# A transformer block on one core: where the projection's products are summed, where the next columns stand, and what a unit's attention waits for

## The chip, the core and the metric

The kernel runs on one core of a Trainium2 chip. The metric is the device time of one execution in microseconds; three runs of the kernel before gave 2201.77 us as the median (2200.89 to 2212.07). All data are 32-bit floats. A product of TensorE (PE in the profile) appears there as two passes, each with its own weight load, so five contraction chunks are "x10".

## The reference

The input `x` is 8 sequences of 512 tokens with 576 features; `cond` is one row of 576 features for each sequence. First the tokens are rotated inside a 64-dimensional subspace: `U` from a QR decomposition of `P`, `R` as the matrix exponential of a skew matrix made from `cond`. Then follows one transformer block whose shifts, scales and gates come from `cond`:

```
x = x + ((x U) R - x U) U^T
ada = silu(c) @ ada_w + ada_b        # six rows of 576: shift, scale, gate, twice
x = x + gate_msa * (attention(modulate(layernorm(x))) @ proj_w + proj_b)
x = x + gate_mlp * mlp(modulate(layernorm(x)))       # 576 -> 2304, gelu, -> 576
```

The attention is unusual: for every token, the 16 heads of that token attend to each other (`einsum('nthd,ntkd->nthk')`), so the scores are 16 x 16 for each token, and no token looks at another. Its result is transposed to heads first and reshaped to rows of 576 before the projection, so a row that is projected mixes 16 tokens of one head.

## The kernel before

**Stages.** A first stage of some 230 us makes the QR decomposition, the exponentials and the modulation. The rest works in 16 **units**, two for each sequence, each of 256 tokens (two tiles of 128). For a unit k the program traces, in this order:

1. `Projection.__init__`: the loads of the projection's weights (L902, L903), of the gathered attention rows `at` (L906) and of the residual rows `x1` (L908), all on SyncE's queue (SP).
2. The **columns** of a later tile: `qkv` gives six pieces for a tile, each a product of 128 tokens with 288 columns over five chunks (L800), copied out of the bank by ScalarE (ACT, L811) and stored to memory (L812). Units 1 to 10 carry the columns of two tiles (12 pieces), units 11 to 14 those of one (6 pieces), unit 15 none; unit 0 carries four pieces. A piece takes its bank from the pool `ps_mm`, which has two.
3. `turn(t)`: five transposes of `at` into banks of `ps_f1`, and two ACT copies to `aT` (L918).
4. `product(t, n)`: four in all, each of five chunks (L928). Before the change their banks also come from `ps_mm`. VectorE (DVE) takes each out with the gate (L930, tile `pt`) and adds it to `x1` (L931).
5. `norm(t)`: statistics on DVE (L137 to L139), a power on GpSimd (POOL, L140), the normalised rows `xn`/`xm` on DVE (L141).
6. `turn_normed`: ten transposes (L946) and five ACT operations that give `h2T` (L949), the input of the MLP.
7. `mlp`: nine steps of fc1 (L973), Gelu on ACT (L981), four sums on POOL (L1029 to L1032; the last is `s3s[g]`), and fc2 (L1044, L1046, L1049) into four banks of `ps_acc`; then nine products into a bank of `ps_f1` (L1059, `p7`); then the **tail**: an ACT copy (L1074), a chain of DVE operations that empties the banks (L1075 to L1087), POOL's additions into `x1` (L989) and the stores `out<-x` (L992). Inside the MLP, `aside` computes the rotation and the transposed input of the sequence two ahead.
8. `ops(40, att)`: all the operations of the attention of unit k+1. Each is a DVE operation on 128 x 2304 elements: eight pairs of product and sum for the scores of both tiles (L838, L845), eight for the values (L866, L873), with a small softmax between.

**What sets the order.** Up to the end of unit 0's projection the orders of PE, DVE and POOL are as the program is written. After that the framework's scheduler makes the order of each engine when the program is built: in its own simulation it gives an engine the earliest traced of the instructions that are ready, and the engines and the SP queue then run these orders strictly. An operation traced late, as the attention's are, so fills any gap that the simulation sees.

**What holds the attention back.** `attention` is a generator. With `after` it first copies one column of some tile into its score tile (L831), so that no sum of scores (L845) can come before that tile exists. Line 1212 gives it `pr.aT[0]`. The lambda is read when the generator starts, which is an iteration later: the attention of unit k+2 waits for `aT[0]` of unit k+1.

```
        if k + 2 < N:
            att = attention(*units[k + 2], after=lambda: pr.aT[0][:, 0, 0:1])
```

**Where the columns stand.** The list of pieces is filled up with `None` in front to twelve entries (L1180). Five stand ahead of `turn(0)`, one between it and `product(0, 0)`, one ahead of each of the other three products, two ahead of the first `turn_normed`, one behind it. A unit with six pieces so has none ahead of `turn(0)` or of `product(0, 0)`.

Of the kernel before, what the change touches and what calls it, by code (L numbers as in the profile page):

```python
# [9 lines left out]
F32 = mybir.dt.float32  # L10
# [14 lines left out]
HALF = D // 2  # L25
# [23 lines left out]
def rotate_then_dit_block(  # L49
# [53 lines left out]
    def srows(c):  # L103
        return 65 if c == 4 else 128
# [47 lines left out]
    with tc.manual_schedule(engines=engines), tc.tile_pool(name="prep", bufs=1) as prep, tc.tile_pool(name="qrs", bufs=2) as qrs, tc.tile_pool(  # L152
        name="ada", bufs=4
    ) as adap, tc.tile_pool(name="exs", bufs=1) as exs, tc.tile_pool(
        name="ps_qr", bufs=1, space=PSUM
    ) as ps_qr, tc.tile_pool(
        name="ps_ex", bufs=2, space=PSUM
    ) as ps_ex, tc.tile_pool(name="ps_m", bufs=2, space=PSUM) as ps_m, tc.tile_pool(
        name="ps_x", bufs=1, space=PSUM
# [374 lines left out]
        t, done = column_products(0), None  # L534
        for j in range(R):
            t, done = qr_step(j, t, done)
# [13 lines left out]
        if True:  # L550
# [43 lines left out]
            for c, rows in enumerate(KROWS):  # L594
                ps = ps_ex.tile([R, 128], F32, tag="ex", name=f"vt_{c}")
# [25 lines left out]
            ps = ps_m.tile([R, R], F32, tag="m", name="s_ps")  # L621
# [38 lines left out]
            for n in range(2):  # L660
                cols = slice(n * HALF, (n + 1) * HALF)
                ps = ps_qr.tile([128, HALF], F32, tag="rp", name=f"first_rot_{n}")
# [9 lines left out]
            for n in range(2):  # L672
                ps = ps_ex.tile([128, HALF], F32, tag="ex", name=f"ut_{n}")
# [15 lines left out]
    ps_mm = ctx.enter_context(tc.tile_pool(name="ps_mm", bufs=2, space=PSUM))  # L689
    ps_f1 = ctx.enter_context(tc.tile_pool(name="ps_f1", bufs=2, space=PSUM))  # L690
    ps_acc = ctx.enter_context(tc.tile_pool(name="ps_acc", bufs=4, space=PSUM))
# [199 lines left out]
    class Projection:  # L891
# [29 lines left out]
        def product(self, t, n):  # L921
            aT, x1 = self.aT[t], x1s[self.hb][t]
            cols = slice(n * HALF, (n + 1) * HALF)
            ps = ps_mm.tile([128, HALF], F32, tag="mm", name=f"pj_{self.hb}_{t}_{n}")
            for c in range(NK):
                k = srows(c)
                w = self.w[n][c // 3][0:k, c % 3]
                nc.tensor.matmul(ps, lhsT=aT[0:k, c, :], rhs=w, start=c == 0, stop=c == NK - 1)  # L928
            tmp = tiles.tile([128, HALF], F32, tag="tmp", name=f"pt_{self.hb}_{t}_{n}", bufs=3)
            nc.vector.tensor_tensor(tmp, ps, self.gate[:, cols], ALU.mult)  # L930
            nc.vector.tensor_tensor(x1[:, cols], x1[:, cols], tmp, ALU.add)  # L931
# [59 lines left out]
    def store(pr, t):  # L991
        nc.sync.dma_start(out=tile_rows(out[pr.b], pr.ts[t]), in_=x1s[pr.hb][t])  # L992
# [20 lines left out]
    def mlp(pr, gate, aside):  # L1013

        hb = pr.hb
        QUARTER = HALF // 2
        gts, sums, s3s = {}, {}, {}
        banks = [ps_acc.tile([128, 512], F32, tag="acc", name=f"fc2_{hb}_{k}") for k in range(4)]
        p = [bank[:, 0:HALF] for bank in banks]
        halves_of = {5: (banks[0], banks[1]), 6: (banks[2], banks[3])}  # L1020
        side = slice(HALF, HALF + QUARTER)
        for g in range(NP + 1):
            if g in aside:
                aside[g]()
            if g < NP:
                gt = gts[g] = fc1(pr, g)
                ss = sums[g] = tiles.tile([128, 3, 128], F32, tag="ss", name=f"ss_{hb}_{g}")
                s3s[g] = tiles.tile([128, 128], F32, tag="s3", name=f"s3_{hb}_{g}", bufs=NP)
                nc.gpsimd.tensor_tensor(ss[:, 0], gt[:, 0, 1], gt[:, 1, 1], ALU.add)  # L1029
                nc.gpsimd.tensor_tensor(ss[:, 1], ss[:, 0], gt[:, 0, 0], ALU.subtract)  # L1030
                nc.gpsimd.tensor_tensor(ss[:, 2], gt[:, 1, 0], ss[:, 1], ALU.subtract)  # L1031
                nc.gpsimd.tensor_tensor(s3s[g], gt[:, 0, 0], gt[:, 0, 1], ALU.subtract)  # L1032
            g -= 1
            if g < 0:
                continue
            wq = wst.tile([128, 3, HALF], F32, tag="w2q", name=f"wq_{hb}_{g}", bufs=3)
            nc.sync.dma_start(out=wq, in_=fc2_q[g])
            wt = wst.tile([128, 3, HALF], F32, tag="w2t", name=f"wt_{hb}_{g}", bufs=3)
            nc.sync.dma_start(out=wt, in_=comb_d[g])
            gt, ss = gts.pop(g), sums.pop(g)  # L1040
            stop = g == NP - 1
            whole = [(gt[:, 0, 0], wq[:, 0]), (gt[:, 1, 0], wq[:, 1]), (ss[:, 2], wq[:, 2]), (gt[:, 1, 1], wt[:, 1])]
            for k in (0, 1, 3):
                nc.tensor.matmul(p[k], lhsT=whole[k][0], rhs=whole[k][1], start=g == 0, stop=stop)  # L1044

            nc.tensor.matmul(p[2], lhsT=whole[2][0], rhs=whole[2][1], start=g == 0, stop=stop)  # L1046
            for i, (lhs, rhs) in ((5, (ss[:, 0], wt[:, 0])), (6, (ss[:, 1], wt[:, 2]))):
                for n, bank in enumerate(halves_of[i]):
                    nc.tensor.matmul(  # L1049
                        bank[:, side],  # L1050
                        lhsT=lhs,
                        rhs=rhs[:, n * QUARTER : (n + 1) * QUARTER],
                        start=False,
                        stop=stop,
                        skip_group_check=True,
                    )
        p7 = ps_f1.tile([128, 512], F32, tag="f1", name=f"p7_{hb}")
        for g in range(NP):
            nc.tensor.matmul(p7[:, 0:HALF], lhsT=s3s[g], rhs=t3[:, g], start=g == 0, stop=g == NP - 1)  # L1059

        def made(tag):
            return tiles.tile([128, HALF], F32, tag=tag, name=f"{tag}_{hb}", bufs=1)

        def add(out_, a, b_, op=ALU.add):

            if isinstance(b_, tuple):
                for n, bank in enumerate(b_):
                    q = slice(n * QUARTER, (n + 1) * QUARTER)
                    nc.vector.tensor_tensor(out_[:, q], a[:, q], bank[:, side], op)
            else:  # L1070
                nc.vector.tensor_tensor(out_, a, b_, op)

        u1, u2, u4 = made("u1"), made("u2"), made("u4")
        nc.scalar.copy(u2, p[0])  # L1074
        nc.vector.tensor_tensor(u1, u2, p[1], ALU.add)  # L1075
        finish(hb, 0, 0, u1, gate)
        add(u2, u2, halves_of[6])
        add(u4, u2, halves_of[5])
        nc.vector.tensor_tensor(u4, u4, p[2], ALU.add)
        finish(hb, 0, 1, u4, gate)  # L1080
        store(pr, 0)
        nc.vector.tensor_tensor(u2, u2, p7[:, 0:HALF], ALU.add)
        c21 = made("u1")
        nc.vector.tensor_tensor(c21, u2, p[3], ALU.subtract)
        finish(hb, 1, 0, c21, gate)
        add(u2, u2, halves_of[5])
        finish(hb, 1, 1, u2, gate)  # L1087
        store(pr, 1)

# [2 lines left out]
    units = [(b, (i, i + 1)) for b in range(B) for i in (0, 2)]  # L1094
    N = len(units)

    def now(pieces):
        for piece in pieces:
            if piece:
                piece()  # L1100

    def ops(n, of):
        for _ in range(n):
# [7 lines left out]
    q = qkv(0, 0)  # L1111
# [6 lines left out]
    q = qkv(0, 1)  # L1118
    att = attention(*units[0])
# [33 lines left out]
    q = qkv(1, 3)  # L1153
# [5 lines left out]
    att = attention(*units[1])  # L1159
    ops(6, att)  # L1160

    ahead = {0: [None] * 5 + q[2:3] + [None] * 3 + q[3:]}
    tiles_of = [(unit[0], i) for unit in units[4:] for i in unit[1]]
    for k in range(1, N - 1):
        for tile_ in [tiles_of.pop(0) for _ in range(2 if k < 11 else 1)]:
# [3 lines left out]
    for k, (b, ts) in enumerate(units):  # L1169
        if ts[0] == 0:  # L1170
            gate_a, gate_m = gate_rows(0, b), gate_rows(1, b)
            gb2 = big.tile([128, D], F32, tag="gb2", name=f"gb2_{b}")
            nc.sync.dma_start(out=gb2, in_=fc2_b.to_broadcast([128, D]))
            nc.gpsimd.tensor_tensor(gb2, gb2, gate_m, ALU.mult)
        pr = Projection(b, ts, gate_a)
        q = ahead.get(k, [])
        if k:
            q = [piece for tile_ in q for piece in qkv(*tile_)]

        q = [None] * (12 - len(q)) + q  # L1180
        now(q[:5])
        pr.turn(0)
        now(q[5:6])
        pr.product(0, 0)
        pr.turn(1)
        now(q[6:7])
        pr.product(0, 1)
        pr.norm(0, gb2)
        now(q[7:8])
        pr.product(1, 0)  # L1190
        now(q[8:9])
        pr.product(1, 1)
        pr.norm(1, gb2)
        if k == 0:
            ops(1, att)
        now(q[9:11])
        pr.turn_normed((0, 1))
        now(q[11:])
        pr.turn_normed((2, 3))
        pr.turn_normed((4,))  # L1200
        if k == 0:
            held.close()
        aside = {}
        if b + 2 < B:
            if ts[0] == 0:
                coming = rotation(b + 2)
            p = coming[:3] if ts[0] == 0 else coming[3:]
            aside = {1: p[0], 3: p[1], 5: p[2], 8: lambda: feature_major(b + 2, ts[0] // 2)}
        mlp(pr, gate_m, aside)
        ops(40, att)  # L1210
        if k + 2 < N:
            att = attention(*units[k + 2], after=lambda: pr.aT[0][:, 0, 0:1])


# [49 lines left out]
```

## Time and profile before

| | us |
|---|---|
| median of three runs | 2201.77 |
| the profiled execution, its own time | 2205.87 |
| its span, first to last instruction | 2204.2 |
| from unit 0's projection on (365 to 2204) | 1839, of which PE is busy 1788.3 |
| period of two units with 12 pieces (L1059 at 960.41, at 1199.29 two units later) | 238.9 |
| period of two units with 6 pieces (L1059 at 1676.76, at 1889.22) | 212.5 |
| one product or one piece (x10, L928 or L800) | about 2.43 |
| one attention operation on DVE (L838, L845, L866, L873) | 2.54 to 2.61 |
| DVE busy in the MLP and projection of one unit (965 to 1083) | 99.2 of 118 |

Shares of busy time: PE 95%, DVE 82%, POOL 32%, ACT 20%. TensorE's granted clock is full from 382 us on, but for seven stretches of 3.4 us at half of full speed in units 12 to 15.

How to read it: in a chain or a timeline, a bracket behind a group gives the idle time ahead of it and what ended that. The number behind a wait is its sum in us, how often it occurred, and the longest.

### The profile page before, as it was taken

How to read it: one execution, taken by the hardware profiler on the slowest of the kernel's cores; microseconds unless marked ns; L12 is line 12 of the kernel's file. 1: busy time of each engine (PE TensorE's matmuls, PEld its weight loads, DVE VectorE, ACT ScalarE, POOL GpSimd, SP SyncE). 2: the span in 40 equal slices, each digit the busy share in tenths (PEclk: the TensorE clock that was granted, in tenths of full speed). 3: DMA queues.
4: the chain of work that ended last, by engine and by line, in shares of the span. 5: the costliest groups of instructions: out<-in, count | busy, mean ns of one | idle time of the engine just before them, and what ended most of it. 6: DMA issues, size and time to landing. Idle time of an engine off the chain costs nothing.

```text
span 2204.2 us, 27929 instructions
## 1 busy us (share of the span) xinstructions
PE 2090.5 (95%) x10087; PEld 1679.3 (76%) x10087; DVE 1801.2 (82%) x2544; ACT 434.9 (20%) x922; POOL 714.1 (32%) x918
## 2 busy tenths in 40 slices
PE   6996998999999999999999999999999999999988
PEld 3475666887878787888878787878787878787867
DVE  8997599788879696969697887969698989896930
ACT  2232221212121111212121212111121212111110
POOL 2341243242424151424333242415142323232422
PEclk9855799999999999999999999999999999999999
DMA  8202265485848576666848484857667676675754
GB/s 272 86 2 73 90 207 158 147 244 160 250 136 244 154 233 191 190 192 199 233 146 252 151 254 132 243 156 230 193 188 221 198 197 184 183 220 166 201 175 124
DMA packets 239789, 400.79 MB, mean 182 GB/s; under 512 B 85502, under 2 KB 127435, under 8 KB 239652
## 3 DMA queue, kind: packets, MB, share of 16 engines
q1 hardware_dynamic: 213732, 372.46, 57.5%
q10 hardware_dynamic: 25920, 26.55, 3.6%
q8 instruction: 80, 1.31, 0.3%
q14 instruction: 57, 0.47, 0.1%
HBM read 340.01 MB, written 58.94 MB: 181 GB/s over the span
## 4 chain that ended last, share of the span: by engine, by line
PE 66%; issue 13%; DVE 9%; POOL 4%; DMA 4%; ACT 3%; SPq 0%; ACTq 0%; POOLq 0%; DVEq 0%
PE fc L973 28%; PE fc L1044 9%; PE qkvp L800 8%; PE fc L1049 6%; PE fc L1046 3%; PE p L1059 2%; PE pj L928 1%; ACT h2T L949 1%; DMA out<-x 1%; DVE sc L845 1%; PE zps L730 1%; PE dp L270 1%; DMA gate<-gates_d 1%; PE ada L352 1%; PE htr L773 1%
## 5 line engine op out<-in xcount | busy, mean ns | idle before, releaser
L973 PE MATMUL fc<-h2T,w 128*128 128x256 f32 (+1 forms) x2880 | 656.5, 382 | 7.3 <-ACT h2T L949 7.2
L973 PEld LDWEIGHTS fc<-h2T,w 128*128 128x128 f32 (+1 forms) x2880 | 542.1, 192 | 83.6 <-ACT h2T L949 11.6
L800 PE MATMUL qkvp<-wqkv,hT 128*128 128x288 f32 (+1 forms) x1920 | 494.1, 412 | 23.6 <-DVE pt L930 15.0
L800 PEld LDWEIGHTS qkvp<-wqkv,hT 128*128 128x128 f32 (+1 forms) x1920 | 365.7, 192 | 130.0 <-DVE pt L930 18.3
L838 DVE TENSOR_TENSOR qk<-qkv 128x2304 f32<-128x2304 f32 x128 | 334.6, 2614 | 12.1 <-DMA qkv<-tok 8.6
L1029 POOL TENSOR_TENSOR ss<-gt 128x128 f32<-128x128 f32 x144 | 155.0, 1076 | 548.3 <-ACT gt L981 548.3
L866 DVE TENSOR_TENSOR pv<-sc,qkv 128x2304 f32<-128x2304 f32 x128 | 330.4, 2581 | 1.8
L873 DVE TENSOR_REDUCE att<-pv 128x144 f32<-128x2304 f32 x128 | 325.8, 2545 | 2.4
L845 DVE TENSOR_REDUCE sc<-qk 128x64 f32<-128x2304 f32 x128 | 325.4, 2543 | 1.7
L981 ACT ACTIVATE gt<-fc 128x512 f32<-128x512 f32 x144 | 86.0, 597 | 649.1 <-PE fc L973 636.5
L811 ACT COPY qs<-qkvp 128x288 f32<-128x288 f32 x180 | 71.9, 399 | 516.7 <-PE qkvp L800 471.1
L1049 PEld LDWEIGHTS fc<-wt,ss 128*128 128x128 f32 x1152 | 160.6, 190 | 15.1
L1049 PE MATMUL fc<-wt,ss 128*128 128x144 f32 x1152 | 164.7, 286 | 0.0
L1044 PE MATMUL fc<-wq,gt 128*128 128x288 f32 x576 | 163.2, 405 | 0.0
L140 POOL TENSOR_TENSOR rstd_m<-rstd_m,mhalf 128x1 f32<-128x1 f32 x32 | 19.6, 613 | 439.4 <-DVE rstd_m L139 369.8
L1044 PEld LDWEIGHTS fc<-wq,gt 128*128 128x128 f32 x576 | 107.5, 189 | 22.7
L1075 DVE TENSOR_TENSOR u<-u,fc 128x288 f32<-128x288 f32 x16 | 7.3, 454 | 136.5 <-ACT u L1074 136.5
L928 PE MATMUL pj<-w2q_p,aT 128*128 128x288 f32 x384 | 104.2, 406 | 0.9 <-ACT aT L918 0.9
L1046 PE MATMUL fc<-wq,ss 128*128 128x288 f32 x288 | 94.1, 408 | 3.2 <-POOL ss L1031 3.2
L1030 POOL TENSOR_TENSOR ss<-ss,gt 128x128 f32<-128x128 f32 x144 | 95.9, 666 | 0.0
L1044 PE MATMUL fc<-wt,gt 128*128 128x288 f32 x288 | 93.4, 406 | 0.0
L831 DVE COPY sc<-aT 128x1 f32<-128x1 f32 x14 | 2.1, 152 | 109.4 <-ACT aT L918 109.4
(254 smaller groups left out, 2393.9 us busy)
## 6 DMA issues: line engine op xcount, KB each, us to landing
w<-in_fc_w SPq DMA_DIRECT2D x288, 320.0 KB
wq<-in_fc_q SPq DMA_DIRECT2D x144, 432.0 KB
wt<-comb_d SPq DMA_DIRECT2D x144, 432.0 KB
tok<-qs ACTq DMA_DIRECT2D x180, 144.0 KB
qkv<-tok SPq DMA_DIRECT2D x30, 864.0 KB
w2q_p<-in_proj_w SPq DMA_DIRECT2D x32, 432.0 KB
xT<-in_x_t SPq DMA_DIRECT2D x16, 640.0 KB
xt<-in_x SPq DMA_DIRECT2D x32, 288.0 KB
```

Source lines behind the costliest of these rows:

```text
L800: nc.tensor.matmul(ps, lhsT=hT[0:k, c, i * 128 : (i + 1) * 128], rhs=wqkv[0:k, c, cols], start=c == 0, stop=c == NK - 1,)
L838: nc.vector.tensor_tensor(pr, q[:, c * HC : (c + 1) * HC].unsqueeze(2).to_broadcast([128, HC, H, DH]), k.unsqueeze(1).to_broadcast([128, H ...
L845: nc.vector.tensor_reduce(sc[t][:, c * HC : (c + 1) * HC, :], pr, AX.X, ALU.add)
L866: nc.vector.tensor_tensor(pr, sc[t][:, c * HC : (c + 1) * HC, :].unsqueeze(2).to_broadcast([128, HC, DH, H]), v.unsqueeze(1).to_broadcast( ...
L873: nc.vector.tensor_reduce(att[:, c * HC : (c + 1) * HC, :], pr, AX.X, ALU.add)
L928: nc.tensor.matmul(ps, lhsT=aT[0:k, c, :], rhs=w, start=c == 0, stop=c == NK - 1)
L973: nc.tensor.matmul(ps[:, k], lhsT=w1[0:n, c, :], rhs=h2T[0:n, c, 0 : NU * 128], start=c == 0, stop=c == NK - 1,)
L1029: nc.gpsimd.tensor_tensor(ss[:, 0], gt[:, 0, 1], gt[:, 1, 1], ALU.add)
L1030: nc.gpsimd.tensor_tensor(ss[:, 1], ss[:, 0], gt[:, 0, 0], ALU.subtract)
L1044: nc.tensor.matmul(p[k], lhsT=whole[k][0], rhs=whole[k][1], start=g == 0, stop=stop)
L1046: nc.tensor.matmul(p[2], lhsT=whole[2][0], rhs=whole[2][1], start=g == 0, stop=stop)
L1049: nc.tensor.matmul(bank[:, side], lhsT=lhs, rhs=rhs[:, n * QUARTER : (n + 1) * QUARTER], start=False, stop=stop, skip_group_check=True,)
```

## The change

Three things change.

- The four products of a projection take their banks from `ps_acc`, the pool of four banks that fc2 accumulates in, not from `ps_mm`.
- The pieces of columns are placed by count: all but the last eight ahead of `turn(0)` (four of 12, none of 6), one ahead of `product(0, 0)`, none between the four products, all but one of the rest ahead of the first `turn_normed` (six of 12, four of 6), the last behind it. Unit 0 keeps the order it had.
- `mlp` returns its list `s3s`, and the attention of unit k+2 waits for `s3s[6]` of unit k's MLP: the fourth POOL sum of the seventh of its nine steps.

```
-            ps = ps_mm.tile([128, HALF], F32, tag="mm", name=f"pj_{self.hb}_{t}_{n}")
+            ps = ps_acc.tile([128, 512], F32, tag="acc", name=f"pj_{self.hb}_{t}_{n}")[:, 0:HALF]
...
-    ahead = {0: [None] * 5 + q[2:3] + [None] * 3 + q[3:]}
+    ahead = {0: q[2:]}
...
-        q = [None] * (12 - len(q)) + q
-        now(q[:5])
+        front = max(0, len(q) - 8)
+        now(q[:front])
         pr.turn(0)
-        now(q[5:6])
+        now(q[front : front + 1])
         pr.product(0, 0)
         pr.turn(1)
-        now(q[6:7])
         pr.product(0, 1)
         pr.norm(0, gb2)
-        now(q[7:8])
         pr.product(1, 0)
-        now(q[8:9])
         pr.product(1, 1)
         pr.norm(1, gb2)
         if k == 0:
             ops(1, att)
-        now(q[9:11])
+        now(q[front + 1 : -1])
         pr.turn_normed((0, 1))
-        now(q[11:])
+        now(q[-1:])
         pr.turn_normed((2, 3))
         pr.turn_normed((4,))
...
-        mlp(pr, gate_m, aside)
+        s3s = mlp(pr, gate_m, aside)
         ops(40, att)
         if k + 2 < N:
-            att = attention(*units[k + 2], after=lambda: pr.aT[0][:, 0, 0:1])
+            att = attention(*units[k + 2], after=lambda s=s3s[6]: s[:, 0:1])
```

`mlp` ends with `return s3s`, and `now` no longer skips empty entries.

More of the change, by code (lines that the diff above doesn't have):

```diff
@@ L1088, in mlp @@
         store(pr, 1)
+        return s3s
     units = [(b, (i, i + 1)) for b in range(B) for i in (0, 2)]
@@ L1098, in now @@
         for piece in pieces:
-            if piece:
-                piece()
+            piece()
     def ops(n, of):
```

## The prediction

> **What bounds the kernel now.** I read the busy shares first, then who waited for whom on PE, then the half-clock stretches, then the timeline of one projection.
>
> ```profile
> PE 2090.5 (95%) x10087; PEld 1679.3 (76%) x10087; DVE 1801.2 (82%) x2544; ACT 434.9 (20%) x922; POOL 714.1 (32%) x918
> ```
>
> PE is the bound: from unit 0's projection on it is busy 1788 of 1839 us. The change removes no product, so only PE's idle time and its slow clock can be won or lost. The waits on PE over the whole span:
>
> ```profile
> engine line waited for: us in total, times, longest us
> ...
> PE qkvp L800 <- DVE pt L930: 15.0, 14, 1.8
> ...
> PE fc L973 <- ACT h2T L949: 7.2, 15, 0.8
> PE h2tr L946 <- DVE xm L141: 6.4, 5, 3.5
> ...
> PE fc L1046 <- POOL ss L1031: 3.2, 6, 0.9
> ...
> PE atr L917 <- DMA at<-att: 2.8, 1, 2.8
> ...
> PE atr L917 <- DVE u L1082: 1.9, 1, 1.9
> ```
>
> The first is the one the change aims at: a piece of columns waits until DVE has taken a product out of one of the two `ps_mm` banks, once in each unit 1 to 14. By stretches, units 1 to 10 wait 0.79 us each and units 11 to 14 1.79 us each (7.9 + 7.2 = 15.1). Units 11 to 14 add waits for `xm` (0.4, 1.1, 1.1, 0.3), and lose clock too; the third number from the end of a windows line is the granted clock (0.92 and 0.84 in unit 13's projection):
>
> ```profile
> 1905.00:1920.00 15.00, 13.21 (x51) 9.93 (x51) 14.55 (x17) 1.20 (x3) 2.10 (x2) 0.92 0.54 168
> 1920.00:1930.00 10.00, 7.64 (x28) 5.46 (x28) 9.45 (x12) 4.80 (x9) 1.96 (x2) 0.84 0.29 87
> ```
>
> Why a bank is taken out late is seen on DVE:
>
> ```profile
> 978.53 0.15 DVE L831 COPY sc<-aT 128x1 f32<-128x1 f32 x1 [10.94 <-ACT aT L918]
> 978.72 2.55 DVE L845 TENSOR_REDUCE sc<-qk 128x64 f32<-128x2304 f32 x1
> 981.31 2.56 DVE L838 TENSOR_TENSOR qk<-qkv 128x2304 f32<-128x2304 f32 x1
> 983.78 0.45 DVE L930 TENSOR_TENSOR pt<-pj,gate 128x288 f32<-128x288 f32 x1
> 984.15 2.54 DVE L845 TENSOR_REDUCE sc<-qk 128x64 f32<-128x2304 f32 x1
> 986.61 0.45 DVE L931 TENSOR_TENSOR x<-x,pt 128x288 f32<-128x288 f32 x1
> 986.97 2.55 DVE L838 TENSOR_TENSOR qk<-qkv 128x2304 f32<-128x2304 f32 x1
> ```
>
> Two things: the copy of L831 holds DVE idle for 10.9 us after the MLP's tail; and once the attention runs, an operation of 2.55 us slips in between two that depend on each other (`pt`, then `x1`).
>
> **The change part by part.** E is the end of the `p7` products.
>
> 1. *Products in `ps_acc`.* They no longer share banks with the pieces, which ACT alone then empties; the five pieces at 964.77 run in 12.31 us with no wait. Units 1 to 10: 10 x 0.79 = **-7.9**. Cost if the cover goes: the four banks must have been emptied by the tail (last read at 967, E + 2; the first product there is at 979.9) and emptied again before fc2, which starts some 9 us behind `h2T`, itself behind the last `pt`. So nothing here.
>
> 2. *Products back to back.* The chain from the last product to its normalised row took 10.6 us in a 12-piece unit (997.6 to 1008.2) and 12.3 in unit 13 (1912.5 to 1924.8). Now more of PE's work stands behind the last product: seven pieces of 2.43 us = 17 us with 12 pieces, which covers the chain; five pieces = 12.2 us with six, which just covers it (unit 11 has 3.5 us of rotation as well). Unit 13 before: E = 1893.4, fc1 starts at 1927.4, E + 34.0. After: 26.5 us of PE work (ten of 2.43 us, two turns of 0.55, ten transposes 1.1) if nothing waits; by the chain: a piece and four products with turns end at E + 14 to 15, + 12.3, + 2.6 from `xm` to fc1 as now = E + 29.5. Gain 4.5, of which 1.8 is the wait for the bank and most of the rest is that the clock stays up.
>    What is there to win in units 11 to 14: bank waits 7.2, `xm` 2.9, `aT` 4 x 0.24 = 0.9, and the half clock: 20 passes of pieces in 6.81 instead of 5.12 us and 40 of fc1 in 10.60 instead of 8.91 (unit 12), about the same in unit 13, 10.44 instead of 8.91 in unit 14: 8.3. Together **19.3**. I take half, **-9.6**, because of part 3.
>
> 3. *Attention from `s3s[6]`.* That sum ends at 1059 where E is 1083: the attention starts some 37 us earlier than now, if the one before has ended. It has: DVE is busy 99 of 118 us a unit, so the hold sets the start and the idle time moves to mid-MLP. The heavy operations now run in the tail: L1075 to L1087 (5.3 us of work on DVE in a dozen operations) get some of them between. Queued behind are POOL's L989, then `out<-x`, and behind that on SP the reload of `x1` (L908 waits for `out<-x` 28 times, 127.6 us). Bounds: no operation more to seven of 2.55 us, 0 to 17.9 us. I take two to three (5 to 7.5 us): several steps are in pairs that need nothing of each other, the `p7` step fills a gap, and the softmax's own small steps fill others. With 12 pieces it is hidden: 9.7 us of pieces and a turn stand ahead of the first product, and `xm` has 3 to 8 us to spare. With six the reload of the second `x1`, issued at 1901.3 (E + 7.9) in unit 13, has 7.4 us until its use at 1911.2 (with 2.5 us for its landing, an estimate between nothing and the 4.6 us that a load three times as large took, 2033.4 to 2038.0), and the turn's fifth transpose waits for L1082 to free `p7` (0.35 us now, up to 2.5 then). This eats the half.
>
> 4. *The last units.* Attention 15 ends at 2101.2, while the tail's ACT copy was done at 2097.3: L1075 is 3.8 us late, PE waits 1.9 us for L1082 and 2.8 us for `at<-att` (2111). It now starts in unit 13's MLP; only its second tile waits, as now, for unit 14's columns (loaded 2033 to 2038). Sixteen operations or 42 us later, 2080, it is done, well ahead. **-4.7**. Between nothing (if both tiles' values also come after the load: 24 operations, 2100) and that.
>
> Added and removed instructions: none on PE or ACT; L831 reads another tile at the same 0.15 us.
>
> Sum: -7.9 - 9.6 - 4.7 = -22.2 on the profiled execution's 2205.9, that is 2183.7; the shown median is 4.1 lower, so the forecast is **2180**.
>
> *A rule against the change.* POOL's sum L1032 takes 448 ns at best, 456 in the median and 2817 at most, the long ones while DVE multiplies; in the last third DVE will multiply. The Trainium skill, "SBUF — State Buffer", section "Who interferes with whom", says that a DVE instruction with two SBUF inputs contends with a GpSimd one that reads SBUF and that a DVE reduction never does; the trace agrees (L1029 takes 2.38 us at 1050.5 under `pv`). It makes the second rival below, whose numbers come from these rows.
>
> **Rivals.**
>
> *Everything is won.* The tail stays short: 15.1 + 2.9 + 0.9 + 8.3 + 4.7 = 31.9, **2170**. For: the sums above. Against: the tail has no cover in six-piece units.
>
> *POOL's sums become the wait.* At the last fc2 step `ss` is needed 4.1 us after Gelu's start (1073.1 to 1077.2) and takes 0.6 + 1.9 us; one multiplication in its way adds up to 2.4, so 0.9 us in each of 15 units: 13. With -7.9 - 4.7 and nothing in six-piece units: about **2202**. For: the six waits of up to 0.9 us on L1031 now. Against: by the order of operations from 1059 on, a multiplication ends near 1074, half a microsecond into the sums, as it does today (0.94 us at 1073.8).
>
> *The attention hardly starts earlier* (loads of its rows, or the order chosen, hold it): parts 1 and a little of 2, **2193**.
>
> *Slower: the tail becomes the path.* Between every two dependent steps of the tail one heavy operation slips in, as in the lines at 983.8. At seven, 17.9 us: the second reload is issued at E + 25.8, `x1` is added at E + 28 instead of E + 17.8, and the 16.3 us from there to fc1 (1911.2 to 1927.4) give E + 44: 10 us more in each of four units, 40 - 7.9 - 4.7 = +27, **2229**. It decides from four to five inserted operations on (4 x (stretch - 7.4) above 12.6, a stretch of 10.5 us). For: that pattern is in every projection. Against: it needs every gap to be filled.
>
> **How the numbers follow.** Forecast 0.45, everything won 0.13, POOL 0.14, no earlier start 0.10, slower 0.18. Half a per cent (11 us) is about what can be told from no change: faster is below 2190.8, slower above 2212.8. Faster: 0.45 + 0.13 = 0.58, the 2193 case on its border; same 0.24; slower 0.18. The forecast's own range is 2168 to 2192 (all or nothing of part 2's half). The range that leaves out 2 in 10 runs from 2165 to 2216: it holds the middle cases and a tail stretched by five operations, not by seven.
>
> **What would show it.** Right: no wait of L800 for `pt`; L831 waits for POOL and not for `aT`, ahead of E by 20 us or more; fc1 of unit 13 starts by E + 30; one half-clock stretch at most in units 12 to 14; no wait for `at<-att` in unit 15. Wrong: more than four heavy operations between L1075 and the last L988 of a tail; the reload of `x1` later than E + 15; a new wait of `h2tr` for `xm` in six-piece units above 4 us; waits of L1046 for `ss` in every unit.

## The result and the profile after

The changed kernel took 2173.2 us in the median of four runs (2170.2 to 2176.1); the kernel before, beside it, 2205.8 us (2200.9 to 2212.1). The ratio is 0.985, with a 95% interval of 0.982 to 0.988: some 33 us faster, where 22 had been forecast. The profiled execution took 2173.5 us with a span of 2171.8, against 2205.9 and 2204.2.

The busy shares of the changed kernel:

```profile
PE 2074.7 (96%) x10087; PEld 1676.4 (77%) x10087; DVE 1825.2 (84%) x2544; ACT 401.4 (18%) x896; POOL 658.7 (30%) x918
```

PE is 16 us less busy with the same 10087 products, part of it by less time at half clock. ACT has 26 instructions less (922 before): all are table loads, 1283 ns each, of which 34 stand beside the softmax (L852) and Gelu (L981) where there were 60. So the prediction's "none on PE or ACT" was wrong for ACT. Every kernel below with the new hold in all units has these 34, and every other has 60; ACT, busy 18% of the span, is not the bound. The waits on PE over the span (us in total, times, longest):

```profile
PE h2tr L946 <- DVE xm L141: 13.1, 12, 3.5
...
PE fc L1046 <- POOL ss L1031: 2.6, 4, 1.6
PE atr L917 <- DMA at<-att: 2.5, 1, 2.5
...
PE fc L973 <- ACT h2T L949: 1.5, 2, 1.3
...
PE atr L917 <- DVE u L1082: 1.2, 1, 1.2
...
PE pj L928 <- DVE u L1079: 0.5, 1, 0.5
```

The first line of before, `qkvp` for `pt`, 15.0 us, is gone altogether. `fc` for `h2T` fell from 7.2 to 1.5. One wait has grown, `h2tr` for `xm`, from 6.4 to 13.1, and it now comes in twelve places instead of five. `at<-att` is still there.

The waits on VectorE show where its idle time went:

```profile
DVE sc L831 <- POOL s L1032: 104.0, 13, 10.4
...
DVE qk L838 <- DMA qkv<-tok: 15.0, 1, 15.0
```

Before, L831 waited 109.4 us in all for `aT`, in ten units just ahead of a projection's products. Now it waits about as long for the POOL sum, in mid-MLP. So most of this idle time is still there, but at another place. The second line has grown: 15 us for one load in unit 14 (8.6 before).

From the start of L1059 in each unit one reads a period for every unit. Summed, in us:

| | before | after | difference |
|---|---|---|---|
| units 1 to 10 (L1059 at 482.93 to 1676.59; after, 481.14 to 1661.86) | 1193.7 | 1180.7 | -12.9 |
| units 11 to 14 (to 2097.47; after, to 2064.12) | 420.9 | 402.3 | -18.6 |
| unit 15 (to 2191.99; after, to 2159.64) | 94.5 | 95.5 | +1.0 |

The 1.8 us that are left lie ahead of unit 0's L1059. That stretch differs by more between executions of one and the same kernel (481.14 here, 485.51 in the repeat below), so nothing is read from it.

The tail in unit 13, where only one piece is traced ahead of the products (start, us, engine, line, operation):

```profile
1870.89 0.45 DVE L1075 TENSOR_TENSOR u<-u,fc 128x288 f32<-128x288 f32 x1
...
1872.81 2.55 DVE L845 TENSOR_REDUCE sc<-qk 128x64 f32<-128x2304 f32 x1
1875.27 0.45 DVE L1079 TENSOR_TENSOR u<-u,fc 128x288 f32<-128x288 f32 x1
...
1876.73 3.02 DVE L838 TENSOR_TENSOR qk<-qkv 128x2304 f32<-128x2304 f32 x1
1879.67 0.45 DVE L988 TENSOR_TENSOR mt<-u,gate 128x288 f32<-128x288 f32 x1
...
1880.46 2.54 DVE L845 TENSOR_REDUCE sc<-qk 128x64 f32<-128x2304 f32 x1
1882.92 0.44 DVE L988 TENSOR_TENSOR mt<-u,gate 128x288 f32<-128x288 f32 x1
```

Three heavy operations have slipped into the tail, the top of the two to three forecast. E is 1873.3; the products run without pieces between them, their last ends near 1886, and fc1 starts at 1903.12, that is E + 29.8 (E + 34.0 before).

### The profile page after: what moved, and what is told of

Same layout as the page of the kernel before. It is cut to its first block, busy times and chain, and to the rows that moved or that the text cites. A ratio compares the mean times of both kernels' runs of the same rounds, so it can differ in the third digit from the quotient of the medians.

```text
span 2171.8 us, 27934 instructions
## 1 busy us (share of the span) xinstructions
PE 2074.7 (96%) x10087; PEld 1676.4 (77%) x10087; DVE 1825.2 (84%) x2544; ACT 401.4 (18%) x896; POOL 658.7 (30%) x918
## 4 chain that ended last, share of the span: by engine, by line
PE 58%; DVE 24%; issue 10%; POOL 4%; DMA 2%; ACT 1%; ACTq 0%; SPq 0%; POOLq 0%; DVEq 0%
PE fc L973 24%; PE fc L1044 8%; PE fc L1049 5%; PE qkvp L800 5%; DVE sc L845 4%; DVE att L873 4%; DVE qk L838 3%; PE fc L1046 3%; DVE pv L866 3%; PE pj L928 2%; PE p L1059 2%; PE zps L730 1%; PE rot L741 1%; PE dp L270 1%; DVE m L325 1%
## 5 line engine op out<-in xcount | busy, mean ns | idle before, releaser
L800 PE MATMUL qkvp<-wqkv,hT 128*128 128x288 f32 (+1 forms) x1920 | 485.0, 410 | 8.0 <-ACT qs L811 5.8
L800 PEld LDWEIGHTS qkvp<-wqkv,hT 128*128 128x128 f32 (+1 forms) x1920 | 364.2, 192 | 110.3 <-ACT qs L811 7.6
L838 DVE TENSOR_TENSOR qk<-qkv 128x2304 f32<-128x2304 f32 x128 | 336.7, 2630 | 18.8 <-DMA qkv<-tok 15.0
L866 DVE TENSOR_TENSOR pv<-sc,qkv 128x2304 f32<-128x2304 f32 x128 | 333.1, 2602 | 2.8
L873 DVE TENSOR_REDUCE att<-pv 128x144 f32<-128x2304 f32 x128 | 326.1, 2548 | 2.6
L1029 POOL TENSOR_TENSOR ss<-gt 128x128 f32<-128x128 f32 x144 | 109.9, 763 | 643.9 <-ACT gt L981 643.9
L981 ACT ACTIVATE gt<-fc 128x512 f32<-128x512 f32 x144 | 86.0, 597 | 769.2 <-PE fc L973 739.9
L989 POOL TENSOR_TENSOR x<-x,mt 128x288 f32<-128x288 f32 x64 | 71.1, 1111 | 211.5 <-DVE mt L988 211.5
L1032 POOL TENSOR_TENSOR s<-gt 128x128 f32<-128x128 f32 x144 | 108.3, 752 | 0.0
L928 PE MATMUL pj<-w2q_p,aT 128*128 128x288 f32 x384 | 104.8, 408 | 0.5 <-DVE u L1079 0.5
L1046 PE MATMUL fc<-wq,ss 128*128 128x288 f32 x288 | 93.9, 408 | 2.8 <-POOL ss L1031 2.6
L831 DVE COPY sc<-s 128x1 f32<-128x1 f32 x14 | 2.1, 153 | 104.0 <-POOL s L1032 104.0
```

What stands on the lines that cost most here:

```text
L800: nc.tensor.matmul(ps, lhsT=hT[0:k, c, i * 128 : (i + 1) * 128], rhs=wqkv[0:k, c, cols], start=c == 0, stop=c == NK - 1,)
L838: nc.vector.tensor_tensor(pr, q[:, c * HC : (c + 1) * HC].unsqueeze(2).to_broadcast([128, HC, H, DH]), k.unsqueeze(1).to_broadcast([128, H ...
L866: nc.vector.tensor_tensor(pr, sc[t][:, c * HC : (c + 1) * HC, :].unsqueeze(2).to_broadcast([128, HC, DH, H]), v.unsqueeze(1).to_broadcast( ...
L873: nc.vector.tensor_reduce(att[:, c * HC : (c + 1) * HC, :], pr, AX.X, ALU.add)
```

## The experiments

The change has three parts: the **banks**, the **columns** and the **hold** (what the attention waits for). All eight combinations of them were run, two kernels that take the columns apart, and three that alter the last unit. A median is compared with that of before in the same group of runs (2207.7, 2205.6 and 2205.7 us). The periods are read as above, each from one profiled execution; a line number behind a tile is that of the kernel shown, and in the kernels with another last order the lines behind the attention stand six further down (L952 is L946).

| kernel | median | ratio to before, 95% interval | units 1-10 | units 11-13 | units 14-15 |
|---|---|---|---|---|---|
| before | 2205.8 | | 1193.7 | 317.8 | 197.6 |
| banks | 2192.8 | 0.994 (0.992 to 0.995) | 1191.0 | 318.3 | 189.5 |
| columns | 2163.6 | 0.981 (0.979 to 0.984) | 1172.3 | 302.0 | 192.7 |
| hold | 2229.7 | 1.011 (1.009 to 1.012) | 1232.3 | 310.7 | 193.0 |
| banks, columns | 2168.3 | 0.983 (0.981 to 0.984) | 1172.3 | 304.2 | 194.0 |
| banks, hold | 2234.5 | 1.013 (1.010 to 1.015) | 1239.7 | 313.6 | 189.9 |
| columns, hold | 2187.9 | 0.991 (0.989 to 0.994) | 1190.5 | 313.1 | 190.5 |
| all three, again | 2173.7 | 0.985 (0.982 to 0.987) | 1180.7 | 307.2 | 190.9 |
| pieces behind only | 2176.0 | 0.987 (0.985 to 0.989) | 1179.6 | 306.7 | 194.6 |
| products together only | 2193.8 | 0.994 (0.993 to 0.996) | 1200.2 | 306.6 | 190.5 |
| all three, last order | 2171.6 | 0.984 (0.982 to 0.987) | 1180.9 | 304.8 | 189.6 |
| banks, columns, hold and order in the last unit only | 2168.0 | 0.982 (0.980 to 0.985) | 1172.3 | 305.7 | 196.9 |
| columns, last order | 2164.0 | 0.982 (0.980 to 0.984) | 1172.2 | 303.9 | 195.6 |

**The banks alone.**

```
-            ps = ps_mm.tile([128, HALF], F32, tag="mm", name=f"pj_{self.hb}_{t}_{n}")
+            ps = ps_acc.tile([128, 512], F32, tag="acc", name=f"pj_{self.hb}_{t}_{n}")[:, 0:HALF]
```

> Only the banks of the four products change (ps_acc in place of ps_mm); the columns stay between the products and the attention waits for aT as before. Theory (cover): the wait of a column for the product's bank (15.1 us in all) goes, but the products and their normalisation chain keep their place, so PE arrives at the transposes of the normalised rows that much earlier and waits there: the h2tr wait for xm grows from 6.4 to some 15 to 20 us, and the time falls by 0 to 5 us only. Rival (banks): the shared banks were the whole cause, the 15 us are won and the time falls by 13 to 17 us.

15.0 us faster, so the total is the rival's. But where it comes from is not what the rival said. In units 1 to 10, where it had 7.9 us to win, the kernel wins 2.7; most of the rest is in the last two units. The waits on PE of this kernel:

```profile
PE h2tr L946 <- DVE xm L141: 24.1, 13, 7.3
...
PE fc L973 <- ACT h2T L949: 5.4, 13, 0.5
...
PE fc L1046 <- POOL ss L1031: 3.0, 7, 0.6
```

The wait for `pt` is gone, and the wait for `xm` went from 6.4 to 24.1 us: PE arrives at `h2tr` earlier and waits there, 0.5 to 1.0 us in each of units 1 to 10 and 18.2 us in units 11 to 15. The theory of cover is right about the mechanism.

**The hold alone**, its line in the diff and `mlp`'s return.

> Only the hold changes: the attention waits for s3s[6], products in ps_mm with columns between them as before. Theory (cover): DVE loses its idle 10.9 us ahead of the projection, but PE's waits for the product's bank stay at 0.8 to 1.8 us a unit; the tail is longer by two to three attention operations; the time lies within 8 us of before. Rival (attention): 15 us or more faster, since DVE's idle time was what the change took away.

22 us slower, which neither theory had. The waits on PE of the hold alone; then from its timeline the products' place on PE, and DVE at the same time:

```profile
PE pj L928 <- DVE pt L930: 21.5, 12, 3.7
...
PE fc L973 <- ACT h2T L949: 7.9, 13, 1.3
PE qkvp L800 <- DVE pt L930: 7.1, 12, 1.4
```

```profile
1246.48 2.59 PE L800 MATMUL qkvp<-wqkv,hT 128*128 128x288 f32 x10
1250.88 1.72 PE L928 MATMUL pj<-w2q_p,aT 128*128 128x288 f32 x6 [1.81 <-DVE pt L930]
```

```profile
1245.13 2.54 DVE L866 TENSOR_TENSOR pv<-sc,qkv 128x2304 f32<-128x2304 f32 x1
1247.59 0.41 DVE L856 TENSOR_REDUCE sm<-sc 128x16 f32<-128x256 f32 x1
1247.91 2.54 DVE L873 TENSOR_REDUCE att<-pv 128x144 f32<-128x2304 f32 x1
1250.37 0.45 DVE L930 TENSOR_TENSOR pt<-pj,gate 128x288 f32<-128x288 f32 x1
```

The product ended at 1246.6 and is taken out at 1250.37, behind two attention operations of 2.54 us each (L866, L873). In the kernel before, VectorE idled 10.94 us for L831 just ahead of the products and took up the attention only 1.4 us before the first of them (978.53 and 979.89). With the hold it works without a gap from mid-MLP through the tail into the products. The spare time is much the same; its place is worse. In units 1 to 10 PE is idle 24.7 us longer than before (40.1 against 15.4) and counts 14.0 us more as busy. Some of the latter is slow clock: this trace has 17.1 us at half clock in these units, where before has none.

**Banks and columns, the old hold.**

> The banks and the placing of the columns as after the change, the attention still held until aT[0] of the next unit. Theory (cover): the normalisation chain now lies under seven or five columns, so both waits go: 12 to 26 us faster than before, and the h2tr wait for xm is not larger than after the change (13 us). Rival (attention): most of the 33 us come from the earlier attention, and this run is less than 8 us faster than before.

39.4 us faster, above the range given: the change without its third part is no slower than the whole. From unit 1 to unit 10 the trace names no wait of PE at all. Units 7 and 8 of this kernel, and then the same two of the kernel before, as windows; the columns are us, PE, PEld, DVE, ACT and POOL busy, granted clock, DMA share, GB/s:

```profile
1186.42:1420.89 234.47, 234.24 (x1106) 193.86 (x1105) 200.13 (x179) 46.82 (x88) 75.45 (x93) 1.00 0.65 201
```

```profile
1199.13:1437.86 238.73, 235.66 (x1107) 193.36 (x1105) 197.71 (x179) 47.46 (x88) 80.78 (x93) 1.00 0.67 198
```

PE idled 3.07 us of 238.73 before and 0.23 of 234.47 here. That is 2.84 of the difference of 4.26; the other 1.4 is time that PE counts as busy. It fits how groups of matmuls join in these traces: without a wait a group starts some 0.16 us before the one ahead has ended (as at 1210.36 in the columns alone below, behind 1208.90 + 1.62), and with a wait it cannot. Each wait would so cost more than its idle time; no run isolates this.

**Columns and hold, products in `ps_mm`.**

> As after the change, but the four products stay in the two ps_mm banks. The products now follow one another 2.43 us apart, and each waits for the take-out of the one two before it, behind attention operations of 2.55 us on DVE. Theory (cover): the third and fourth product and the first column after them wait for pt, 2 to 6 us a unit in the 14 units with columns, so 20 us or more slower than after the change, about as before it or slower. Rival: the scheduler fills these waits with columns and the time is within 8 us of after.

19.9 us faster, some 12 less than the whole change beside before. Without the four banks, PE waits for `pt` again (11.4 us at L928 and 8.7 at L800). So with the columns and the hold in place the banks do pay.

**The columns alone**, the change with before's `ps_mm` and before's hold; with it the whole change again.

> The columns alone out from between the products; banks and hold as before. Theory 'the parts add up' (banks and columns less banks alone, 24 us): 22 to 26 us faster than before. Rival 'without the four banks the products wait for VectorE one after another' (the 1.0 us wait of each unit in columns with the new hold, and more in units 11 to 14): 5 to 12 us faster.

> The change whole, unaltered, beside the next three on one chip. Theory 'the earlier attention is a cost' (banks and columns give all of the gain, and the hold on the POOL sum gives back about 0.8 us in each of units 1 to 10): 4 to 6 us slower than banks and columns with the old hold, so some 33 to 35 us faster than before. Theory 'the earlier attention is a gain that one run hid': 38 us or more faster than before.

The columns alone: 2163.6 us, 42 faster than before, more than either theory had. The repeat of the whole is 32 us faster, as the theory of a costly hold had it. The waits on PE of the columns alone:

```profile
PE h2tr L946 <- DVE xm L141: 7.3, 4, 3.5
...
PE atr L917 <- DMA at<-att: 2.4, 2, 2.0
...
PE qkvp L800 <- DVE pt L930: 2.1, 2, 1.2
```

Units 1 to 10 take 1172.3 us with or without the new banks (1172.27 and 1172.33), with no wait from unit 1 to unit 10. The 15.0 us of waits for `pt` that the banks were to remove are down to 2.1 without them (and 0.9 at L928). The timeline of the columns alone shows why, on PE (the last product and the pieces behind it) and on DVE at that time:

```profile
1208.90 1.62 PE L928 MATMUL pj<-w2q_p,aT 128*128 128x288 f32 x6
1210.36 1.14 PE L928 MATMUL pj<-w2t_p,aT 128*128 128x288 f32 x4
1211.33 14.01 PE L800 MATMUL qkvp<-wqkv,hT 128*128 128x288 f32 x57
```

```profile
1199.70 0.15 DVE L831 COPY sc<-aT 128x1 f32<-128x1 f32 x1 [8.51 <-ACT aT L918]
...
1208.14 0.45 DVE L930 TENSOR_TENSOR pt<-pj,gate 128x288 f32<-128x288 f32 x1
...
1209.24 0.45 DVE L930 TENSOR_TENSOR pt<-pj,gate 128x288 f32<-128x288 f32 x1
...
1212.93 0.45 DVE L930 TENSOR_TENSOR pt<-pj,gate 128x288 f32<-128x288 f32 x1
```

With the products side by side, their small DVE operations come in a row, and the scheduler puts few heavy ones between them. Both banks are free when the next piece wants them. One number shows it in all traces: from the end of a product on PE to the start of its L930 it takes, in the mean of units 1 to 10, 1.6 us where pieces stand between the products and the hold is the old one (with or without the new banks), 1.1 us where none do, and 2.1 to 2.9 us with the new hold.

**The columns taken apart.** First the pieces go behind the second norm, but in the units with 12 pieces one stays between each two products (before's kernel with `[:1]`, `[1:2]`, `[2:3]`, `[3:4]`, `[4:5]`, `[5:11]` for the first six places); then the products stand together, but eight pieces lie ahead of the first transpose and a ninth ahead of the first product:

```
-        front = max(0, len(q) - 8)
+        front = max(0, len(q) - 4)
```

> Before's banks and hold, and a column still between each two products; only the counts move: of 12 pieces of a unit one instead of five lies ahead of the first transpose, and six instead of two between the second norm and the transposes of the normed rows. Theory 'cover' (what the columns gain is that four more pieces, 9.7 us of TensorE, hide the chain from the last product to xm and h2T): most of the gain of the columns alone, 30 to 42 us faster than before. Rival 'contiguity' (what gains is that no column piece takes a product's bank in turn): within 8 us of before.

> Before's banks and hold; no column between the products, as in the columns alone, but eight pieces ahead of them and two behind the second norm, as many behind as before had. Theory 'cover': TensorE reaches the transposes before xm of the second tile (12 us behind the last product in the columns alone) and waits 3 to 8 us in each of units 1 to 10 on top of what before lost, so the run is between 10 us faster and 40 us slower than before. Rival 'contiguity': 30 to 42 us faster than before, like the columns alone.

Pieces behind only: 30 us faster, just below the range of the theory of cover (30 to 42); in units 1 to 10 it wins 14.1 of the 21.4 us of the columns alone, and what it keeps is before's wait for `pt`, here in its timeline on PE:

```profile
1218.96 6.34 PE L800 MATMUL qkvp<-wqkv,hT 128*128 128x288 f32 x25 [0.77 <-DVE pt L930]
```

Products together only: 12 us faster, just outside what the theory of cover gave and far from the rival's 30 to 42, which falls. Its waits for `xm` are only 0.7 to 0.9 us in units 5 to 10, less than the 3 to 8 that theory asked for, and units 1 to 10 lose 6.5 us. So in units 1 to 10 the cover carries two thirds, and taking the pieces out from between the products adds the rest (7.3 us) only once the cover is there.

**Banks and hold, columns as before.**

> The banks and the hold on the POOL sum, columns as before: the last corner of the three parts. Theory 'the banks pay for what the hold does' (the hold alone lets VectorE come late to the products' banks, 2.3 us of waits for pt in a unit; four banks take that away, and nothing else is lost): as the banks alone within 8 us, 7 to 23 us faster than before. Rival 'the hold's price lies also in xm, ahead of which no more cover lies than before': slower than before by 0 to 15 us.

29 us slower: the rival's sign and place, but twice its size, and the theory that the banks pay for the hold falls. This kernel's timeline at `h2tr`, PE and then DVE:

```profile
1278.09 1.54 PE L946 MATMUL h2tr<-ident,xm 128*128 128x128 f32 x6 [3.71 <-DVE xm L141]
```

```profile
1275.01 2.54 DVE L873 TENSOR_REDUCE att<-pv 128x144 f32<-128x2304 f32 x1
1277.47 0.57 DVE L141 TENSOR_SCALAR xm<-x,mv_m,rstd_m 128x576 f32<-128x576 f32 x1
```

The wait for `pt` has become one for `xm`, 37.2 us over the span, at the other end of the same chain. The banks can only move such a wait; whether it is then covered is up to the columns.

Much of the size that the rival lacked is slow clock. Here are units 1 to 10 as a window, of banks and hold and then of the banks alone; the clock is the third number from the end:

```profile
481.01:1720.75 1239.74, 1196.03 (x5522) 978.60 (x5521) 1021.84 (x900) 212.01 (x421) 325.48 (x465) 0.98 0.63 192
```

```profile
479.22:1670.18 1190.96, 1176.47 (x5523) 966.36 (x5522) 993.02 (x892) 236.54 (x440) 419.66 (x465) 1.00 0.65 198
```

Of the 48.8 us between them 19.6 are PE's busy time with the same products. In each of these ten units a half-clock stretch of 3.4 or 6.8 us lies at the wait for `xm`, 44.4 us in all; at half speed that is up to 22 us of lost work, an estimate from these stretches.

**The last unit's attention in another order**: the values of its first tile ahead of the scores of the second.

```
+        if b == B - 1 and ts[0] == 2:
+            shares(0)
+            yield from values(0)
+            yield from scores(1)
+            raised(1)
```

> The change whole, with one edit: in the last unit's attention the values of the first tile come ahead of the scores of the second, whose input is loaded late, so that VectorE need not idle 14.96 us for that load. Theory 'the last unit loses to that load alone': its attention ends at least 6 us earlier, L1075 then waits for the ACT copy, the wait at<-att (2.5 us) and the wait of PE for L1082 (1.2 us) go, and the run is 4 to 5 us faster than the change whole. Rival 'the idle VectorE was the cover of unit 14': with it filled, the projection of unit 14 waits for xm again (1.9 us and its ACT waits, as with the old hold), half to all of it is given back, and the run is 0 to 2 us faster.

The medians differ by 2.2 us, which the intervals don't tell apart, but the traces show both claims at work. Unit 15 takes 89.5 us instead of 95.5, its wait for `at<-att` gone. Unit 14 takes 100.2 instead of 95.1. From the timelines: the load that VectorE waited for in the whole change; then VectorE at the same place with the other order; then PE there:

```profile
2003.94 2.56 DVE L838 TENSOR_TENSOR qk<-qkv 128x2304 f32<-128x2304 f32 x1 [14.96 <-DMA qkv<-tok]
```

```profile
1994.00 0.58 DVE L141 TENSOR_SCALAR xm<-x,mv_m,rstd_m 128x576 f32<-128x576 f32 x1 [0.44 <-POOL rstd_m L140]
1994.49 2.54 DVE L873 TENSOR_REDUCE att<-pv 128x144 f32<-128x2304 f32 x1
1999.14 2.56 DVE L838 TENSOR_TENSOR qk<-qkv 128x2304 f32<-128x2304 f32 x1 [2.10 <-DMA qkv<-tok]
```

```profile
1994.63 0.39 PE L952 MATMUL h2tr<-ident,xm 128*128 128x128 f32 x1 [2.30 <-DVE xm L141]
```

The idle VectorE was unit 14's cover. Filled with values, it hands `xm` over late. Of the 5.0 us that unit 14 loses, 1.7 are PE's idle time and 3.3 its busy time: a half-clock stretch of 6.8 us lies at this wait.

**Two attempts at a faster kernel.** Banks and columns with the new hold and order for the last attention only:

```
+            att = attention(*units[k + 2], after=(lambda s=s3s[6]: s[:, 0:1]) if k == N - 3 else lambda: pr.aT[0][:, 0, 0:1])
```

> Banks and columns with the old hold in all units but the last, whose attention is held on the POOL sum and has the order of the run before. From the period of each unit in the traces so far (units 1 to 10 as with the old hold, 1172.3 us; units 11 and 12 206.3; unit 13 98 to 100; unit 14 95.1 if its cover stays, 99.5 if not; unit 15 90 to 91), theory 'the earlier attention is a cost where the kernel is full and a gain only at the end': 10 to 13 us faster than the change whole. Rival 'the cover of unit 14 goes': 5 to 8 us faster than the change whole, no more than banks and columns with the old hold.

The columns alone, with the new order:

> The columns alone, and the last unit's attention with the values of the first tile ahead of the scores of the second. VectorE idles only 2.0 us for the load there, so its attention can end at most some 2 us earlier. Theory: the wait at<-att (2.0 us) and PE's wait for L1082 (1.2 us) go and unit 14 keeps its 99.4 us: 2 to 4 us faster than the columns alone, 38 to 46 us faster than before. Rival 'what unit 15 wins, unit 14 loses', as in the change whole: as the columns alone within 2 us.

The first is 5.7 us faster than the whole change, the rival's number: unit 14 takes 106.0 us, with 10.2 us at half clock. The second is at the columns alone (2164.0 and 2163.6): unit 14 goes from 99.4 to 102.5 us, unit 15 from 93.3 to 93.0. So the columns alone stay the fastest kernel of this study by median, some 10 us ahead of the whole change (2163.6 and 2173.7 in one group of runs). Their intervals, 0.979 to 0.984 and 0.982 to 0.987, just overlap, but with the new columns and banks units 1 to 10 take 1180.7 to 1180.9 us in all three traces with the new hold there and 1172.3 in both with the old one. Banks and columns together are not told apart from the columns alone.

## Why the prediction was right, and where it was not

The forecast of 2180 us was 7 too high, and the time lies inside its range of 2168 to 2192. The direction was right; the sum came near because errors cancelled, which is luck. By its terms:

- **Units 1 to 10, -7.9 for the banks.** Measured -12.9. The size of the wait was right: it is worth 7.3 us (pieces behind only, against the columns alone). But the columns remove it by themselves, and with before's columns the banks turn it into a wait for `xm` and win 2.7. The banks are worth 9.8 us only behind the new hold (1190.5 against 1180.7), where they win back half of what it costs.
- **Part 2, the columns' cover in units with 12 pieces.** The prediction named the seven pieces behind the last product and gave them no price in these units. This is the term that was most mis-sized: 14.1 us. `fc` for `h2T` (0.5 us in a unit) and for `ss` (0.5 in every other) were in the prediction's list of waits, but in no term; both are gone with the pieces behind. They are half of it. The other half, 6.5 us, is PE's busy time, which the prediction held fixed but for the clock.
- **Part 3, "With 12 pieces it is hidden".** This step failed. In the whole change the hold costs 8.4 us in units 1 to 10 (1180.7 against 1172.3 with the old hold), 18.2 without the banks, 38.7 alone, the last with slow clock in it. Three operations in the tail were foreseen rightly, but the price is not paid in the tail: it is paid at `pt` and `xm`, where VectorE now takes a product out 2.1 to 2.9 us after its end instead of 1.1 to 1.6. The reason, read from the timelines and tested only with these two holds, is that VectorE no longer comes to the products straight out of an idle gap: its 10.4 us for L831 now lie in mid-MLP.
- **Units 11 to 14, -9.6, half of 19.3.** Measured -18.6, nearly all. fc1 of unit 13 at E + 29.8 against 29.5 worked out, the reload of `x1` at E + 14.4, inside the E + 15 allowed: the working was right, the halving was not. But part of that is luck. Against the columns alone, units 11 to 13 of the whole change lose 5.1 us (307.1 and 302.0), so the hold had a cost there, and unit 14 wins 4.3 back (95.1 and 99.4). Unit 14 gives 7.9 of the 18.6, and the experiment with the order shows that 5.0 of these hang on the idle wait for the load, which the prediction did not have. Of the five half-clock stretches in these units one is left.
- **The last unit, -4.7.** Measured +1.0. The bound that the prediction named held: both tiles' values come after the load. L1075 starts at 2067.05, behind the attention, where ACT's copy was done at 2064, and `at<-att` stays at 2.5 us. The unit also has 10.2 us at half clock in place of 6.8, which can be up to 1.7 us, an estimate from these stretches.

Of the rivals, "everything is won" had the nearest time (2170) by a wrong route. POOL's sums did not become the wait: 2.6 us for `ss` on L1046 in all. The rule cited on shared SBUF ports showed elsewhere, in this line of the costliest groups of the changed kernel (busy us and mean ns behind the first bar):

```profile
L989 POOL TENSOR_TENSOR x<-x,mt 128x288 f32<-128x288 f32 x64 | 71.1, 1111 | 211.5 <-DVE mt L988 211.5
```

The additions that follow the tail take 1111 ns in the mean and 3045 at most, where all 64 took 791 to 803 before. Nine of them take 3.04 us, and each of the nine begins while an L838 runs. The L838 at 1876.73 in the tail above, which starts behind such an addition (1876.53), took 3.02 instead of 2.55 us. The Trainium skill, "SBUF — State Buffer", section "Who interferes with whom", has a DVE instruction with two SBUF inputs contend with a GpSimd one that reads SBUF, and the trace agrees.

The slower rival, the tail as the path, did not come: three operations, not seven. But a slowdown by the hold was real; it was hidden by the other two parts.

What is not settled: whether the overlap of the matmuls is all of the 1.4 us by which PE's busy time falls in two units, and how the hold's price runs with its place. Only `aT[0]` and `s3s[6]` were tried, no sum between.

## What to carry to other kernels

Run the parts of a change alone before keeping them together: here one of three gave all of the gain by itself, the second was worth something only where the others left a wait, the third cost time, and the sum hid it. A wait removed at one end of a dependent chain comes back at its other end unless independent work stands there to cover it, so look for the cover first. And idle time on an engine that is not the bound can be what makes it prompt: before filling it or moving it, see whose operations come right behind the gap.

## What the runs showed of the hardware that had not been expected

TensorE's half clock came after waits shorter than the 3.4 us for which it lasts, and not after every one. In unit 12 the whole change waited 2.30 us for `xm` and then ran at a granted clock of 0.69 in the window shown first. Its repeat did the same (2.31 us, and 3.4 us at half clock). The whole change with the other last order, whose source differs only in the last unit's attention, waited 2.24 us there and kept its clock, as its window below shows. The length of the wait alone does not decide it: in the kernel before, the same wait of 1.79 us stands in each of units 11 to 14, and a half-clock stretch follows it at once in units 12 and 13 (at 1811.9 and 1917.7) but not in 11 and 14. What else decides is not shown. The columns are those of the windows above; the third number from the end is the clock.

```profile
1795.00:1800.00 5.00, 3.37 (x9) 2.43 (x10) 4.97 (x7) 1.40 (x3) 1.40 (x1) 0.69 0.01 2
```

```profile
1795.00:1800.00 5.00, 5.00 (x27) 4.00 (x26) 4.96 (x6) 3.20 (x7) 1.01 (x1) 1.00 0.10 31
```

The periods of that unit are 103.0 us (in both executions of the whole change) and 100.6. So a difference of some 2.4 us in units 11 to 14 between two kernels' profiles can be one half-clock stretch, and has to be read with the clock beside it.
